# A normalisation with four times the variance and a Newton step that gives twice its result: one GpSimd scaling fewer in each of 51

## The chip, the cores and the metric

The kernel runs on one core of a Trainium2 chip. The metric is the device time in microseconds (us) of one execution; lower is better. It is one launch, all in 32-bit floats.

## The reference, cut to what matters

The input `x` has the shape 128 batches x 64 steps x 256 features. Two blocks follow each other. The first is a linear attention with a modulated output; the second a selective state-space scan (Mamba) over permuted steps. Three layer normalisations stand in them, and they are all that the change touches:

```python
def _layernorm(x, scale, bias):
    mu = jnp.mean(x, axis=-1, keepdims=True)
    var = jnp.var(x, axis=-1, keepdims=True)
    return (x - mu) * jax.lax.rsqrt(var + LN_EPS) * scale + bias      # LN_EPS = 1e-5
# block 1
xn = _layernorm(x, norm_scale, norm_bias)            # then q, k, v = xn @ W + b
...                                                  # softmaxes, k^T v, q (k^T v) -> y
h = _layernorm(y, film_norm_scale, film_norm_bias) * (1.0 + scale) + shift
x = x + silu(h) @ film_out_W + film_out_b
# block 2
h = _layernorm(x, gamma, beta) * (1.0 + scale) + shift
h = h[:, perm]
xm, z = split(h @ W_in)                              # conv over 4 steps, silu
dt = softplus(xm @ W_xp[:, :64] @ W_dt + b_dt);  Bm, Cm = xm @ W_xp[:, 64:]
hst = hst * exp(dt * A) + dt * xm * Bm;  ys = sum(hst * Cm)           # over the 64 steps, 512 x 16 states
x = x + gate * ((ys + xm * D_param) * silu(z) @ W_out)[:, inv_perm]
```

## The kernel before, in words

The 128 batches are worked in 16 groups of 8 (512 rows, four tiles of 128 rows). For a group, `prepare` (line 831) does everything up to the inputs of the scan, `scan` (line 1094) does one half of the group's state-space scan, and `finish` (line 1179) the output of that half. The first group is prepared in two parts of two tiles each (`first0`, `first2`), so there are 17 calls of `prepare`, and each calls `normalise` (line 757) three times: for `xn` from the input (line 855), for `yn` from the attention's result (line 984) and for `x1` from the first block's output (line 997). That is 51 normalisations, 45 on four tiles and 6 on two.

A normalisation has four stages. VectorE takes `bn_stats` of each tile into `st`: for the even and the odd features apart it gives a mean (`m0`, `m1`) and a sum of squares about it (`s0`, `s1`). GpSimd works on small tiles of 128 partitions x 4 (or x 2): `dm` is the difference of the two means, squared and scaled by a quarter; `ve` is the sum of squares over 256 plus epsilon; their sum is the variance. ScalarE takes the logarithm of `ve` and the exponential of minus half of it, which gives a first `r0` near the reciprocal root. GpSimd then makes one Newton step, `rt = r0 * (1.5 - 0.5 * r0 * r0 * ve)`, and the shift `mu = -mean * rt`. Last, ScalarE applies `rt` and `mu` to each tile in the four `Identity` activations.

The heavy work of a group lies elsewhere, and all engines share it. For each half of a group and each of four blocks of channels, TensorE makes the scan's input `hb` from `uT` and `diag`, ScalarE makes the decays (`decay`, eight exponentials for each buffer), VectorE runs the scan (1024 elements a partition), GpSimd or VectorE multiplies by `ct`, GpSimd adds one half of the states to the other, and TensorE folds the result into `yacc`. GpSimd also makes `diag` (line 1106) from `bT`, which ScalarE copies at line 1055 at the end of a chain of projections (`xp`, `zp`, `pd`, `bp`) of the next group.

The order of the work is written out by hand. Nothing is issued as the functions run; a planner (`Plan`, line 407 on) records every operation as a node. `order` (line 431) gives each node a due time, the later of its entry in the table `ORDER` (one list for each function, one entry for each node in the order of recording, plus 100000 for each group) and the due times of the nodes it needs:

```python
at[n] = max([ORDER[name][i] + PERIOD * g] + [at[m] for m in n.needs])
```

Nodes are then issued in the order of their due times, a little later where a buffer is missing. Each engine's queue runs strictly in that order. So the prepare of group g+1 is interleaved with the scan of group g, and the normalisations `yn` and `x1` of one group and `xn` of the next come within some 25 us of each other. Every operation passes through one line of the planner's `emit` (line 485), so the profile names nearly everything L485; the tiles' names tell the operations apart. Tables of ScalarE's functions are loaded at line 481.

Of the kernel before, what the change touches and what calls it, by code (L numbers as in the profile page):

```python
# [12 lines left out]
ALU = mybir.AluOpType  # L13
# [4 lines left out]
B, T, D, E = 128, 64, 256, 512  # L18
# [21 lines left out]
EPS = 1e-5  # L40
# [25 lines left out]
        -999921, -996486, -990765, -972941, -999936, -1000000, -999905, -999936, -999936,  # L66
        -990323, -998987, -999758, -1000000, -987539, -988111, -966277, -971501, -986083,
        -957916, -994987, -986377, -974444, -950200, -952896, -986046, -972526, -957682,
        -979289, -987850, -970490, -949297, -916289, -985408, -963837, -941730, -952038,
        -930967, -907453, -907447, -928120, -884449, -861711, -935360, -959099, -906197,  # L70
        -884745, -926919, -902673, -909643, -906909, -906200, -908429, -898155, -903063,
        -813008, -868162, -912159, -899153, -999936, -997120, -990221, -999936, -1000000,
        -999792, -826771, -682771, -989347, -990592, -990016, -992211, -992211, -978429,
        -982690, -440858, -484572, -442918, -404750, -431762, -406261, -406938, -370644, 453,
        -324628, -326712, -958581, -421254, -324629, -325398, -324629, -324629, -387488,
        -324629, -844574, -838288, -326191, -325953, -324629, -324456, -325371, -319531,
        -301212, -300329, -164417, -391164, -172529, -301121, -167816, -288749, -164473,
        -231435, -167985, -147673, -163941, -164313, -139790, -307173, -146289, -147223,
        -139567, -174994, -164473, -134847, -144594, -150226, -134317, -144822, -146906,
        -134316, -147826, -134386, -140173, -134315, -152590, -134805, -134707, -133013,  # L80
        -326287, -190004, -131686, -200375, -133015, -207481, -996027, -132927, -129988,
        -147732, -133273, -106986, -885223, -132530, -108249, -140659, -133037, -101338,
        -974289, -116497, -107952, -133014, -130547, -100436, -588731, -67587, -68642,
# [3 lines left out]
        -999784, -999756, -822479, -813355, -999773, -991829, -999405, -993980, -992161,  # L87
        -994087, -999400, -768764, -665327, -621700, -817491, -634769, -637890, -583888,
        -627342, -663883, -601358, -457294, -523956, -446498, -782722, -556542, -717683,
        -582039, -586409, -433401, -454285, -421287, -459329, -497809, -425655, -426154,  # L90
        -429164, -419967, -387487, -419719, -321626, -293880, -406937, -361628, -497357,
        -426940, -411887, -350269, -394780, -374539, -327849, -288748, -335565, -299633,
        -264048, -247552, -231344, -219423, -553809, -433515, -461393, -441827, -423327,
        -431823, -153333, -156188, -454096, -424751, -304161, -258938, -279273, -283415,
        -340857, -144850, -134706, -131268, -136899, -155056, -134271, -136435, -433892, -62033,
        -475762, -434892, -554380, -465884, -328157, -510237, -384539, -628574, -121233,
        -121771, -500934, -906743, -472740, -164647, -181881, -164481, -754360, -116569,
        -109561, -121834, -105660, -135210, -104940, -106021, -75578, -66547, -80773, -68153,
        -144505, -98818, -104252, -89186, -77436, -94044, -86891, -73823, -74895, -77276,
        -108505, -98473, -96861, -86338, -75448, -53191, -48981, -52833, -52458, -53800, -68746,  # L100
        -53712, -52940, -53192, -48477, -47718, -100418, -38381, -36696, -47354, -48108, -92558,
        -19487, -8631, -41476, -47273, -43456, -162871, -49575, -12810, -35339, -42049, -44442,
        -99823, -55773, -24279, -22535, -47650, -47276, -147956, -23424, -9283, -17974,
# [42 lines left out]
        -149966, -147998, -147736, -150000, -150000, -149540, -149273, -150000, -149489,  # L146
        -150000, -150000, -147255, -150000, -143483, -147722, -149580, -150000, -141887,
        -145855, -141886, -143290, -141594, -149567, -147693, -143761, -142133, -138763,
        -147418, -149815, -141646, -141865, -149377, -148702, -141774, -140597, -150000,
        -148702, -139206, -142860, -148144, -141417, -148704, -139302, -141567, -141330,  # L150
        -143545, -147601, -138501, -138860, -137760, -149965, -149390, -137567, -132849,
        -141748, -138950, -138764, -138744, -134769, -129564, -138764, -129760, -147721,
        -133650, -136715, -138641, -129765, -128205, -117699, -119220, -122722, -123478,
        -111005, -111004, -119884, -111271, -119852, -116230, -113143, -111005, -111114,
        -111004, -112111, -111005, -148865, -143220, -111005, -111005, -122959, -122926,
        -122986, -100655, -100656, -103176, -104256, -115077, -102238, -115728, -100658, -97964,
        -99626, -97970, -104665, -125773, -96887, -96913, -98002, -101766, -105253, -97787,
        -97126, -97126, -97126, -97126, -98335, -98054, -140963, -150000, -96888, -97126,
        -100461, -96556, -96888, -94054, -94132, -94053, -94133, -85309, -88765, -85234, -95423,
        -76351, -77623, -68358, -77139, -68709, -73881, -69122, -66121, -75878, -88439, -77322,  # L160
        -105836, -102274, -88194, -88979, -74881, -112072, -68758, -100829, -65194, -53340,
        -68359, -52170, -68869, -53341, -67392, -52171, -67165, -43786, -67246, -35127, -116295,
        -47828, -34648, -46451, -34171, -61735, -121472, -9650, -13197, -9791, -53250, -34170,
        -104935, -145568, 491, -21442, 22014, -32279, -29845, -106976, -20621, -8465, -1812,
        -19172, -29844, -36753, -25168, -3093, 7305, 15576, 11066,
# [39 lines left out]
        -150000, -148365, -149379, -148186, -147710, -148145, -150000, -147883, -147449,  # L205
        -141333, -146678, -149293, -137329, -142658, -146045, -137210, -150000, -129185,
        -138016, -129063, -150000, -122022, -137245, -146237, -134166, -119944, -107662,
        -114443, -146460, -119822, -142594, -125518, -149605, -117748, -107503, -116280,
        -115986, -101530, -105490, -101792, -108496, -111964, -113055, -119580, -142326,
        -135091, -113196, -106219, -110898, -119052, -117009, -109071, -104082, -115434,  # L210
        -101155, -101587, -101160, -102995, -101154, -121691, -107621, -118019, -98668, -103562,
        -110841, -96160, -94342, -106883, -96129, -88496, -93851, -88453, -86210, -87882,
        -73554, -79765, -149134, -125438, -137689, -117745, -149723, -145371, -73501, -77699,
        -148135, -149745, -103126, -103183, -77189, -81922, -148511, -68983, -67148, -66564,
        -71719, -56737, -55081, -61739, -55082, -60951, -49107, -56022, -47710, -75024, -47619,
        -48170, -47523, -47522, -48365, -47884, -53314, -48195, -49047, -47523, -46123, -47711,
        -73484, -55695, -47450, -44286, -47523, -47450, -44286, -42413, -42179, -41790, -41791,
        -30440, -31655, -30010, -29626, -24609, -34436, -25715, -25899, -47788, -27114, -28689,
        -26119, -35153, -29556, -27554, -27234, -69385, -44266, -44072, -24078, -27966, -20537,
        -44394, -44754, -22794, -26297, -95547, -21060, -23242, -22793, -55083, -24610, -23243,  # L220
        -19275, -23836, -34187, -16800, -21249, -15031, -14288, -111162, -13874, -6687, -22973,
        -21580, -14543, -14287, -149968, -7150, 866, -553, -314, -14542, -14286, -150000,
        -13685, 3873, 17012, 16186, -14374, -14286, -148362, -2118, 7814, 17635, 39067,
    ],
    "scan0_last": [
# [263 lines left out]
def block_kernel(  # L489
# [33 lines left out]
    pl = Plan(tc)  # L523
# [233 lines left out]
    def normalise(dst, src):  # L757
# [7 lines left out]
        mu, ve, dm = (small(a, [P, n]) for a in ("mu", "ve", "dm"))  # L765
# [12 lines left out]
        rt = small("rt", [P, n])  # L778
# [501 lines left out]
```

## Time and profile before

| | us |
|---|---|
| device time, median of 3 runs (lowest to highest) | 1947.62 (1947.34 to 1949.36) |
| device time of the profiled execution | 1950.4 |
| its span, first to last instruction | 1948.7 |
| TensorE busy (matmuls) | 1825.3 |
| GpSimd busy | 1788.3 |
| VectorE busy | 1776.0 |
| ScalarE busy | 1698.9 |
| the 51 scalings `dm<-dm` by a quarter on GpSimd, by their durations | 8.8 + 1.2 |

PE is TensorE's matmuls, PEld its weight loads, DVE VectorE, ACT ScalarE, POOL GpSimd. In a row of the groups, `out<-in` are the tiles written and read, then their shapes and how many there are, then the busy time, the mean duration of one in ns, and the engine's idle time just ahead of them with what ended most of it. In a row of the timeline the first number is the start in us from the span's start and the second the length of the row; a row may merge several like instructions, and square brackets give the idle time ahead and who ended it. A wait row names the waiting engine and tile, the one that released it, the total in us, the number of waits and the longest. The profiled execution is the one in which all these are measured; its device time is 2.8 us above the median of the runs.

### The profile page before, as it was taken

The numbers are of one execution on the slowest core, as the hardware profiler recorded it, in microseconds if no ns is written. First come the engines' busy times: TensorE is split into PE (matmuls) and PEld (weight loads), VectorE is DVE, ScalarE is ACT, GpSimd is POOL, SyncE is SP. The second block draws the span as 40 slices with busy tenths as digits, with TensorE's granted clock in tenths as the row PEclk, the third lists the DMA queues.
The fourth block names the chain that finished last, engine by engine and source line by source line (L and its number), as shares of the span: only waits on it lengthen the run. The fifth ranks groups of instructions, "written<-read, shape, count | busy, mean of one in ns | idle before, by whom it ended". The sixth has DMA issues, their size and how long they took to land. (4 is left out here: it accounts for less than half of the span.)

```text
span 1948.7 us, 32432 instructions
## 1 busy us (share of the span) xinstructions
PE 1825.3 (94%) x11304; PEld 931.1 (48%) x11304; DVE 1776.0 (91%) x1626; ACT 1698.9 (87%) x3981; POOL 1788.3 (92%) x1519
## 2 busy tenths in 40 slices
PE   6798999999999999999999999999999999999777
PEld 5453544545455454545535454453545445454233
DVE  5589799999999999999999999999999999999796
ACT  5889799898989989899998989889898998989762
POOL 3579799999999999999999999999999999999997
PEclk9899999999999999999999999999999999999898
DMA  4211322204122221412213132220412222041220
GB/s 142 80 50 45 85 72 73 82 23 120 39 86 64 67 87 28 112 54 85 64 56 88 38 103 61 81 68 28 115 39 86 72 68 84 23 114 36 82 65 22
DMA packets 173083, 135.71 MB, mean 70 GB/s; under 512 B 30804, under 2 KB 157000, under 8 KB 172920
## 3 DMA queue, kind: packets, MB, share of 16 engines
q1 hardware_dynamic: 172920, 133.64, 23.7%
q8 instruction: 90, 1.47, 0.3%
q14 instruction: 73, 0.60, 0.1%
HBM read 98.84 MB, written 34.75 MB: 69 GB/s over the span
## 5 line engine op out<-in xcount | busy, mean ns | idle before, releaser
L485 DVE TENSOR_TENSOR_SCAN hs<-decay,hb 128x1024 f32<-128x1024 f32 x384 | 864.0, 2276 | 69.4 <-PE hb L485 21.8
L485 ACT ACTIVATE decay<-dt,nA 128x252 f32<-128x252 f32 x2048 | 859.2, 503 | 77.1 <-DMA dt<-dt_d 40.5
L485 POOL TENSOR_TENSOR hs<-hs,ct 128x1024 f32<-128x1024 f32 x384 | 900.1, 2366 | 20.6 <-DVE hs L485 16.2
L485 PE MATMUL hb<-diag,uT 64*64 64x512 f32 x4096 | 534.5, 619 | 67.9 <-DVE hs L485 63.0
L485 POOL TENSOR_TENSOR hs<-hs 128x1024 f32<-128x1024 f32 x224 | 526.6, 2364 | 13.8 <-DVE hs L485 9.9
L485 DVE TENSOR_TENSOR_SCAN hb<-decay,hb 128x1024 f32<-128x1024 f32 x128 | 291.7, 2279 | 0.0
L485 PE MATMUL yacc<-hs,fold 128*64 128x256 f32 x2304 | 283.5, 387 | 4.3 <-ACT yacc L485 2.2
L485 PEld LDWEIGHTS hb<-diag,uT 64*64 64x64 f32 x4096 | 122.1, 133 | 294.7 <-DVE hs L485 125.6
L485 PEld LDWEIGHTS yacc<-hs,fold 128*64 128x64 f32 x2304 | 163.3, 137 | 123.3 <-issue 49.7
L481 ACT ACT_TABLE_LOAD x160 | 205.3, 1283 | 3.5 <-PEq L1268 0.8
L485 DVE TENSOR_TENSOR hs<-hb,ct 128x1024 f32<-128x1024 f32 x128 | 156.3, 1221 | 5.1
L485 DVE SCALAR_TENSOR_TENSOR xz<-xp,vec,xz 128x504 f32<-128x504 f32 (+5 forms) x204 | 140.8, 701 | 12.1 <-ACT xz L485 7.5
L485 POOL TENSOR_TENSOR diag<-fold,bT 128x1024 f32<-128x1024 f32 x64 | 122.1, 1909 | 10.3 <-ACT bT L485 10.3
L485 PE MATMUL zp<-h,win 128*128 128x512 f32 (+1 forms) x272 | 123.4, 580 | 1.6 <-DVE xz L485 0.6
L485 PE MATMUL xp<-h,win 128*128 128x512 f32 (+1 forms) x272 | 118.3, 578 | 2.1 <-DVE xz L485 1.1
L485 PE MATMUL yop<-wout,xz 128*128 128x256 f32 x512 | 117.6, 383 | 0.0
L485 PEld LDWEIGHTS yop<-wout,xz 128*128 128x128 f32 x512 | 94.7, 190 | 25.1 <-ACT decay L485 10.6
L485 POOL TENSOR_TENSOR w<-dt,xz 128x512 f32<-128x512 f32 (+1 forms) x68 | 81.7, 1212 | 12.9 <-ACT dt L485 12.4
L485 ACT ACTIVATE yacc<-xz,vec 128x256 f32<-128x256 f32 x128 | 60.1, 470 | 32.7 <-PE yacc L485 32.7
L485 PEld LDWEIGHTS xp<-h,win 128*128 128x128 f32 x272 | 50.7, 192 | 68.8 <-issue 50.7
L485 PEld LDWEIGHTS zp<-h,win 128*128 128x128 f32 x272 | 48.6, 189 | 62.4 <-issue 43.5
L485 ACT ACTIVATE hT<-htp,mods 128x64 f32<-128x64 f32 x256 | 77.9, 441 | 0.2
(138 smaller groups left out, 2358.8 us busy)
## 6 DMA issues: line engine op xcount, KB each, us to landing
ct<-c_d SPq DMA_DIRECT2D x128, 256.0 KB
dt<-dt_d SPq DMA_DIRECT2D x256, 128.0 KB
dt_d<-dt SPq DMA_DIRECT2D x60, 256.0 KB
ga<-gate_d SPq DMA_DIRECT2D x64, 128.0 KB
xr<-x_d SPq DMA_DIRECT2D x32, 256.0 KB
out<-xr SPq DMA_DIRECT2D x32, 256.0 KB
xt<-in_x SPq DMA_DIRECT2D x15, 512.0 KB
x_d<-xt SPq DMA_DIRECT2D x15, 512.0 KB
```

The source lines that it names most:

```text
L481: engine.preload_act_table_set(loaded)
L485: getattr(engine, method)(*real, **kreal)
```

## The change

The quarter ahead of the sum goes: `ve` becomes four times the variance (and four times epsilon), so `dm` squared is added as it is. ScalarE's `r0` is then half the reciprocal root, and the Newton step with the constants -1 and 3 in place of -0.5 and 1.5 gives twice its usual result, which is the reciprocal root itself. One instruction of GpSimd is left out in each normalisation; two others get other constants.

```diff
         pl.gpsimd.tensor_tensor(dm, m0, m1, op=ALU.subtract)
         pl.gpsimd.tensor_tensor(ve, s0, s1, op=ALU.add)
         pl.gpsimd.tensor_tensor(dm, dm, dm, op=ALU.mult)
-        pl.gpsimd.tensor_scalar(ve, ve, 1.0 / D, EPS, op0=ALU.mult, op1=ALU.add)
-        pl.gpsimd.tensor_scalar(dm, dm, 0.25, 0.0, op0=ALU.mult, op1=ALU.add)
+        pl.gpsimd.tensor_scalar(ve, ve, 4.0 / D, 4.0 * EPS, op0=ALU.mult, op1=ALU.add)
         pl.gpsimd.tensor_tensor(ve, ve, dm, op=ALU.add)
         r0 = small("r0", [P, n])
         pl.scalar.activation(r0, ve, AF.Ln)
...
         pl.gpsimd.tensor_tensor(rt, r0, r0, op=ALU.mult)
         pl.gpsimd.tensor_tensor(rt, rt, ve, op=ALU.mult)
-        pl.gpsimd.tensor_scalar(rt, rt, -0.5, 1.5, op0=ALU.mult, op1=ALU.add)
+        pl.gpsimd.tensor_scalar(rt, rt, -1.0, 3.0, op0=ALU.mult, op1=ALU.add)
         pl.gpsimd.tensor_tensor(rt, rt, r0, op=ALU.mult)
```

The table `ORDER` loses the entries of the nodes that are gone, three in each of the lists `first0`, `first2`, `second` and `prepare` (so 172 entries become 169, and 202 become 199); every other entry keeps its value. The start of `prepare`:

```diff
     "prepare": [
         -150000, -150000, -143902, -149054, -149244, -148364, -149973, -150000, -148365,
-        -150000, -148365, -149379, -148186, -147710, -148145, -150000, -147883, -147449,
+        -150000, -148365, -148186, -147710, -148145, -150000, -147883, -147449, -141333,
```

## The prediction, made before the changed kernel was run

> **What bounds the kernel now.** I read the page first: busy shares, the 40 slices, the groups. They show no single bound.
>
> ```profile
> PE   6798999999999999999999999999999999999777
> DVE  5589799999999999999999999999999999999796
> ACT  5889799898989989899998989889898998989762
> POOL 3579799999999999999999999999999999999997
> ```
>
> From the seventh slice (290 us) to the 37th, TensorE, VectorE and GpSimd all stand at nine tenths; ScalarE is just under. So a busy share names no bound; the order of the hand-overs must. In the page's chain that ended last there is nothing before 1803 us, so I followed the hand-overs by hand through the timeline of one group, 1128 to 1243 us. GpSimd's `diag` that waits for `bT` marks the same place in every group: it starts at 1127.95 and 1243.14, 115.19 us apart. The list of waits comes next.
>
> ```profile
> ACT r L485 <- POOL ve L485: 58.4, 36, 6.8
> POOL diag L485 <- ACT bT L485: 10.3, 13, 0.8
> ```
>
> ScalarE waits for the normalisations' `ve` 36 times, 58.4 us in all, and GpSimd waits for ScalarE's `bT` once a group. So GpSimd hands to ScalarE, and ScalarE back to GpSimd. What lies between is shown by the timeline of the group.
>
> ```profile
> 1164.59 0.20 POOL L485 TENSOR_TENSOR dm<-st 128x4 f32<-128x4 f32 x1 [0.20 <-DVE st L485]
> 1164.74 0.21 POOL L485 TENSOR_TENSOR ve<-st 128x4 f32<-128x4 f32 x1
> 1164.89 0.20 POOL L485 TENSOR_TENSOR dm<-dm 128x4 f32<-128x4 f32 x1
> 1165.19 0.20 POOL L485 TENSOR_SCALAR ve<-ve 128x4 f32<-128x4 f32 x1
> 1165.47 0.20 POOL L485 TENSOR_SCALAR dm<-dm 128x4 f32<-128x4 f32 x1
> 1165.75 0.20 POOL L485 TENSOR_TENSOR ve<-ve,dm 128x4 f32<-128x4 f32 x1
> 1165.90 0.20 POOL L485 TENSOR_TENSOR mu<-st 128x4 f32<-128x4 f32 x1
> ...
> 1189.43 0.20 ACT L485 ACTIVATE r<-ve 128x4 f32<-128x4 f32 x1 [0.95 <-POOL ve L485]
> ...
> 1191.31 2.07 ACT L485 ACTIVATE x<-xt,mu,rt 128x256 f32<-128x256 f32 x4 [0.25 <-POOL mu L485]
> ...
> 1193.43 1.60 PE L485 MATMUL gtp<-gsel,x 128*128 128x128 f32 x12 [0.17 <-ACT x L485]
> ...
> 1196.63 2.29 DVE L485 TENSOR_TENSOR_SCAN hs<-decay,hb 128x1024 f32<-128x1024 f32 x1 [0.88 <-ACT decay L485]
> ...
> 1243.14 1.90 POOL L485 TENSOR_TENSOR diag<-fold,bT 128x1024 f32<-128x1024 f32 x1 [0.78 <-ACT bT L485]
> ```
>
> The reader is to see a ring. From 1164.59 (`dm` of `yn`) to 1192 GpSimd is never released by another engine: it works through `yn` (1164.59 to 1167.8), large multiplications, and `x1` with `xn` interleaved (1186.57 to 1192.3). ScalarE waits 0.95 us for the last `ve` and 0.25 us for `mu`. From there ScalarE stands in unbroken work until `bT` at 1242.84, save for a wait of 0.17 us later. TensorE (0.17), VectorE (0.88) and finally GpSimd (0.78) wait for it. The other side closes it: TensorE waits 0.43 us for ScalarE's `xz` at 1222.02 and then runs without a stop to the `hb` for which VectorE waits 0.30 us at 1248.76; in the group before, the same VectorE stretch (from 1133.57, with one wait of 0.32 us for TensorE's `ap`) ends in the `st` for which GpSimd waits 0.20 us at 1164.59. All three normalisations of a group lie on this ring.
>
> **The change part by part.** *The instruction that goes* is the row `dm<-dm` at 1165.47. Its duration is 0.20 us (the two groups of them: 45 of 196 ns and 6 of 196 ns, with 3.6 and 0.4 us idle ahead of them). But its place in the queue is longer: 1165.19, 1165.47, 1165.75 are starts 0.28 us apart, while a following independent instruction starts 0.15 us on (1165.75, 1165.90). After the change `ve<-ve,dm` follows `ve<-ve`, on which it depends as it depends on the squared `dm`, so one step of 0.28 us goes, not 0.15: that is my value, since before and after the next neighbour is a dependent one. In the interleaved pair, `x1` at 1187.16, 1187.43 and `xn` at 1188.65, 1188.92, the step is 0.27. The Trainium skill's page "Perfetto Trace Analysis", section "GPSIMD Engine Instruction", says that the span reported for a GpSimd instruction can't be relied on and that starts of consecutive instructions should be used. The rows bear that out: neighbours' spans overlap (1165.75 + 0.20 is past 1165.90) where they are independent, and have gaps where they aren't. By the reported spans the 51 instructions would come to 10.0 us, by the spacing to 14.3 us.
>
> *The two other constants* are operands of instructions that stay; 0 us. *The order*: the lists lose just the entry of the node that goes, and a due time is the later of the entry and the needs. The entry decides for its successor in one list alone, `second`, -147736 against -147998 for `ve`, a shift of 0.26 us of plan time in one group, and no other node of GpSimd or ScalarE lies between. So every queue keeps its order, no DMA and no wait is moved, and nothing is added.
>
> *What lies on the path.* Thirteen times (yn at 243, 358, 473 ... 1627 us, each with `x1` and `xn` some 22 us later) three scalings lie on the ring: 3 x 0.277 = 0.83 us a time. Whether all of it comes through hangs on what is late next, which for the case of 1189 us can be read:
> - VectorE's own way to 1196.63 has a slack of 0.88 us, just above 0.83.
> - TensorE's `hb` at 1190.67 follows VectorE (1.71 us of waiting, which GpSimd does not touch); then `rp` and `gtp`. `gtp` starts at 1192.66, and its end gains at most some 0.43 us: the `hb` after it starts at 1194.97, where 1192.66 and the 1.88 us of an unhindered `gtp` (1769.54 to 1771.42, where it waits for nothing) give 1194.54. But the second `xtp`, 1198.94, waits again for ScalarE's `h`: `yacc` ahead of it takes 2.32 us in place of 1.88 to 1.95, so TensorE catches up the missing 0.4 us there.
> So I take the whole 0.83 us in the ten groups like this one. In three (610 to 620, 1071 to 1081, 1303 to 1313 us) the granted clock is 0.83 in a window of 10 us just here, where the other ten show 1.00. The `gtp` then takes 2.91 to 3.14 us and TensorE, not ScalarE, sets the second `xtp`. Groups between two `diag` marks last 114.83 us at the least; the two that hold a single such window, 115.59 and 115.35 (one without it, 782 to 898 us, lasts 115.62, so the clock isn't the only cause). So 0.5 to 0.76 us of another delay lies beside the ring there, and of 0.83 us I count 0.25.
>
> The sum, against the profiled execution of 1950.4 us: ten groups x 0.83 = 8.3; three x 0.25 = 0.8; the last group's `yn` and `x1` (1742, 1764 us) 2 x 0.28 = 0.55; the first half's `xn`, `yn`, `x1` (6, 29, 49 us), where ScalarE waits 6.8, 2.8 and 1.4 us for `ve`, all on the serial start, 3 x 0.28 = 0.85; the seven others between 26 and 200 us, where GpSimd also waits up to 5.9 us for VectorE, at half, 1.0. Together **11.5 us**: 1938.9 in that execution, which is 2.8 above the median of 1947.62, so **1936.1** as a median. Floor and ceiling of what is not known: none of it comes through (0), or all 51 steps do (14.3 us) and the three slow-clock windows go away as well (3 x 0.6 = 1.8): 1931.5.
>
> **The rivals.**
> 1. *TensorE's way through `gtp` is late next.* If the catch-up at `xtp` doesn't happen, a group gains the 0.43 us that TensorE can gain there. For it: `gtp`'s wait is only 0.17 us in the row shown, and TensorE is busy without a pause afterwards. Against: the stretched `yacc`. 10 x 0.43, nothing in the three slow-clock groups, and 1.6 of start and end: 5.9 us, 1941.7.
> 2. *The wait only changes hands.* If the ring is closed by VectorE or TensorE work that I haven't seen as such, ScalarE's waits for `ve` (0.95 and 2.3 us a group) and GpSimd's for `st` and `bT` grow by what is saved, and the gain stays at the start, 1 to 2 us: 1946. For it: TensorE, VectorE and GpSimd are each idle only some 4 to 5 us a group. That the change moves an instruction's work to its neighbour and so saves only the 0 to 0.15 us of dispatch would look much the same.
> 3. *Slower: the clock.* A window at the lower clock falls on the same pause of TensorE in 3 of 13 groups; it is seen as 0.66 over 1075 to 1080 us, which is 1.7 us of TensorE's work. If a tighter ScalarE chain moved the pause so that it is caught in all 13, and TensorE became the bound with the full 1.7 us on the path, the ten new ones cost 17 us against 11.5 gained: 1953. It decides from nine new windows on ((11.5 + 3.9) / 1.7). Against it: the pause itself, 1.71 us before the `hb` at 1190.67, comes from VectorE and keeps its length, and `gtp`'s wait gets shorter. The skill's page "TensorE: Matmul & The Clock Gate", section "What's actually happening", says that the clock is lowered after an idle window of about 3.4 us that runs free of the kernel; no idle time of TensorE that long stands in these rows, so by the page the pause would cost nothing, and where the windows fall would be chance.
>
> **How the numbers follow.** The forecast has 62%, rival 1 20%, rival 2 14%, rival 3 4%. The predicted time is the forecast's, 1936.1. The range takes in the forecast with the bound of 1931.5 and rival 1 (1941.7) with some 2 us for its own spread: 1931.5 to 1944, which leaves out rivals 2 and 3, 18%. About 0.2%, 3.9 us, is what a measurement of this kernel can tell from no change. Faster by more: forecast and rival 1, 82%; within: rival 2, 14%; slower by more: 4%.
>
> **What would show it.** GpSimd has 51 instructions fewer (1468) and 10 us less busy time. `ve<-ve,dm` starts 0.28 us after `ve<-ve`. The marks of `diag` lie some 114.0 us apart in an undisturbed group, against 114.83. GpSimd's waits for `bT` (0.79) and `st` (0.2) stay as they are; VectorE's 0.88 shrinks to near 0.05. If the step is mis-sized, the waits of ScalarE for `ve` keep their length and the marks move by less; under rival 1 TensorE's wait at `gtp` is gone and no stretched `yacc` is left; under rival 2 the waits grow by 0.8 us a group. I am wrong most easily in the slack: 0.88 against 0.83 us is a hair, read in one group.

## The result, and the profile after

The changed kernel takes 1939.48 us (median of five, 1936.99 to 1942.74) against 1947.62 us (five, 1945.41 to 1951.31) of the kernel before on the same chip: a ratio of 0.9959, with a 95% interval from 0.9944 to 0.9974. That is 8.1 us less, where 11.5 were forecast. Beside two more sets of runs of the kernel before, the changed kernel gave 0.9950 [0.9933, 0.9968] and 0.9937 [0.9923, 0.9951], by the medians 9.7 and 12.6 us less. Its profiled execution took 1942.74 us, its span 1941.0: 7.7 us less than the profiled one of before.

The page of the changed kernel, in 40 slices, shows the same picture as before, since no busy share tells of a ring:

```profile
PE   7799999999999999999999999999999999999777
...
DVE  4589799999999999999999999899999999999796
ACT  4889799898989989899898989889898998989762
POOL 3589799999999999999999999999999999999997
```

Its list of waits (engine and tile that waits, who released it, total in us, how often, the longest):

```profile
ACT r L485 <- POOL ve L485: 44.4, 32, 6.2
...
POOL dm L485 <- DVE st L485: 34.5, 19, 5.9
...
POOL diag L485 <- ACT bT L485: 10.2, 13, 0.8
```

ScalarE's wait for the normalisations' `ve` fell from 58.4 to 44.4 us; GpSimd's wait for `bT` stayed at 13 times 0.79.

The timeline of the changed kernel, at the places that were shown of before (start, length, engine, tiles, and in brackets the idle time ahead with who ended it):

```profile
1161.10 0.20 POOL L485 TENSOR_TENSOR dm<-st 128x4 f32<-128x4 f32 x1 [0.20 <-DVE st L485]
...
1161.70 0.20 POOL L485 TENSOR_SCALAR ve<-ve 128x4 f32<-128x4 f32 x1
1161.98 0.20 POOL L485 TENSOR_TENSOR ve<-ve,dm 128x4 f32<-128x4 f32 x1
1162.13 0.20 POOL L485 TENSOR_TENSOR mu<-st 128x4 f32<-128x4 f32 x1
...
1183.49 0.19 POOL L485 TENSOR_SCALAR ve<-ve 128x4 f32<-128x4 f32 x1
1183.77 0.21 POOL L485 TENSOR_TENSOR mu<-st 128x4 f32<-128x4 f32 x1
1183.92 0.20 POOL L485 TENSOR_TENSOR ve<-ve,dm 128x4 f32<-128x4 f32 x1
...
1184.82 0.19 POOL L485 TENSOR_SCALAR ve<-ve 128x4 f32<-128x4 f32 x1
1185.10 0.20 POOL L485 TENSOR_TENSOR ve<-ve,dm 128x4 f32<-128x4 f32 x1
...
1185.33 0.21 ACT L485 ACTIVATE r<-ve 128x4 f32<-128x4 f32 x1 [0.37 <-POOL ve L485]
...
1187.20 2.08 ACT L485 ACTIVATE x<-xt,mu,rt 128x256 f32<-128x256 f32 x4 [0.24 <-POOL mu L485]
...
1189.17 1.95 PE L485 MATMUL gtp<-gsel,x 128*128 128x128 f32 x16
...
1192.52 2.29 DVE L485 TENSOR_TENSOR_SCAN hs<-decay,hb 128x1024 f32<-128x1024 f32 x1 [0.26 <-ACT decay L485]
...
1192.65 2.13 PE L485 MATMUL yacc<-hs,fold 128*64 128x256 f32 x16
...
1238.99 1.90 POOL L485 TENSOR_TENSOR diag<-fold,bT 128x1024 f32<-128x1024 f32 x1 [0.79 <-ACT bT L485]
```

Of the kernel before, the first normalisation of the pair, and TensorE's `yacc`:

```profile
1187.16 0.19 POOL L485 TENSOR_SCALAR ve<-ve 128x4 f32<-128x4 f32 x1
...
1187.43 0.19 POOL L485 TENSOR_SCALAR dm<-dm 128x4 f32<-128x4 f32 x1
1187.58 0.21 POOL L485 TENSOR_TENSOR mu<-st 128x4 f32<-128x4 f32 x1
...
1187.74 0.20 POOL L485 TENSOR_TENSOR ve<-ve,dm 128x4 f32<-128x4 f32 x1
...
1196.57 2.32 PE L485 MATMUL yacc<-hs,fold 128*64 128x256 f32 x16
```

Here is where the time went. The yn at 1161 us has its sum 0.28 us after `ve<-ve`, where it was 0.56 (1165.19 to 1165.75). In the pair, the first normalisation is xn (of the next group) and the second is x1; the prediction named the two the other way round. x1's sum (1185.10) also comes 0.28 after `ve<-ve`. In xn, however, `mu<-st` has moved into the free place, so the sum comes 0.43 after `ve<-ve` (before, 1187.16 to 1187.74, it was 0.58): 0.15 saved, not 0.28. Together 0.28 (yn) + 0.27 (x1, where it was 0.55) + 0.15 (xn) = 0.70 us a group. ScalarE's wait for the last `ve` is 0.58 us shorter, TensorE no longer waits in `gtp`, and VectorE's wait for `decay` shrank from 0.88 to 0.26.

The `diag` marks give it for the whole execution:

| distances of the 13 marks, us | shortest | all twelve together | first mark | from the last mark to the end |
|---|---|---|---|---|
| before | 114.83 | 1383.86 | 321.67 | 243.2 |
| changed | 114.13 | 1377.89 | 321.98 | 241.1 |
| changed, second profile (a later run) | 114.16 | 1377.24 | 319.99 | 242.1 |
| changed, third profile (a later run) | 114.15 | 1376.18 | 321.53 | 239.9 |

The shortest distance fell by 0.67 to 0.70 us. The twelve together lost 6.0 to 7.7 us; twelve times 0.70 would be 8.4. Two distances of the first profile grew: the sixth (115.47, before 114.83) and the ninth (117.99, before 116.65). In each lies a spell at half the clock (at 958 and at 1255 us) that the kernel before doesn't have there. The timeline of TensorE in the sixth:

```profile
956.53 1.09 PE L485 MATMUL hb<-diag,uT 64*64 64x512 f32 x8 [1.71 <-DVE hs L485]
957.55 1.68 PE L485 MATMUL rp<-yo,gsel 128*128 128x256 f32 x4
959.02 3.09 PE L485 MATMUL gtp<-gsel,x 128*128 128x128 f32 x16
```

Against 1.13 and 1.95 us for the same `rp` and `gtp` at 1188 to 1191 us, the spell costs TensorE 1.7 us; the group's mark comes some 1.3 us later than in an undisturbed group (114.13).

One more wait tells how long a group is. Some 9 us behind its mark, ScalarE's `decay` waits for `dt`, which has gone out to memory and comes back by DMA. In the changed kernel's fourth and fifth group (114.14 and 114.99 us):

```profile
673.62 2.88 ACT L485 ACTIVATE decay<-dt,nA 128x252 f32<-128x252 f32 x7 [1.17 <-DMA dt<-dt_d]
...
788.61 2.88 ACT L485 ACTIVATE decay<-dt,nA 128x252 f32<-128x252 f32 x7 [2.03 <-DMA dt<-dt_d]
```

In groups at the shortest distance this wait is 0.9 to 1.2 us. Where it is longer, and no spell at half the clock lies in the group, the distance is the shortest one plus what the wait has above 1.17 us: here 114.13 + 0.86 = 114.99, and in the kernel before 114.83 + 0.78 = 115.61, measured 115.62 (782 to 898 us). Over the twelve profiles this holds within 0.04 us in 110 of 112 such groups (the first of each profile is left out; it is 0.1 to 0.5 us longer than that); in 101 of them the profile puts the wait down to this DMA, in the others to VectorE's `qm` or `qt`. In the sixth group a wait of 1.41 us takes 0.24 of the 1.34 us and leaves 1.1 for the spell. So a group lasts as long as the ring, plus a late `dt`, plus a spell. The change shortened the first by 0.67 to 0.70; the other two differ from profile to profile, and the sum over the twelve distances with them. No run altered the trip of `dt`, so its part is read from the rows and not tested.

### The profile page after: what moved, and what is told of

The parts are those of the page before. It is cut to its first block, busy times and chain, and to the rows that moved or that the text cites. A ratio compares the mean times of both kernels' runs of the same rounds, so it can differ in the third digit from the quotient of the medians.

```text
span 1941.0 us, 32381 instructions
## 1 busy us (share of the span) xinstructions
PE 1819.4 (94%) x11304; PEld 931.0 (48%) x11304; DVE 1775.8 (91%) x1626; ACT 1696.5 (87%) x3981; POOL 1778.1 (92%) x1468
## 5 line engine op out<-in xcount | busy, mean ns | idle before, releaser
L485 POOL TENSOR_TENSOR hs<-hs,ct 128x1024 f32<-128x1024 f32 x384 | 899.5, 2363 | 19.9 <-DVE hs L485 14.8
L485 POOL TENSOR_TENSOR diag<-fold,bT 128x1024 f32<-128x1024 f32 x64 | 122.0, 1907 | 10.2 <-ACT bT L485 10.2
```

The costliest lines, as they stand in the source:

```text
L485: getattr(engine, method)(*real, **kreal)
```

## The experiments

The theory, **A**: what counts is GpSimd time ahead of the sums that release ScalarE, since ScalarE's chain sets the pace of a group. A rival, **B**: GpSimd is full, and its time counts wherever it lies. Another, **C**: something else is late next, so only a part comes through. All marks below are the shortest distance between two `diag`; in the two kernels that were profiled more than once it differs by 0.03 to 0.04 us.

**The changed kernel again.** No edit.

> The changed kernel as it is, timed again. Both theories: 5 to 11 us under the kernel before. What it tells apart is the spread: if the start of the trace and the groups with a lower granted clock differ from execution to execution, the shortest distance of two diag marks is again 114.13 us (0.02 either way) while the first diag mark and the longer distances move by up to 2 us. If instead the change itself moved the start by 1 us (the dm at 243.07 us before stood at 244.17 after), the first marks come at the same place as in the first profile.

Measured: 1940.68 us (1934.54 to 1948.66, seven runs), ratio 0.9950; marks 114.16. The gain is there again, with marks 0.03 us from the first; the first mark moved by 2.0 us, and single executions scatter by several us.

**The quarter left out in one normalisation only** (one execution each). The edit, for one of the three sites:

```diff
+        f = 4.0 if site == here else 1.0
-        pl.gpsimd.tensor_scalar(ve, ve, 4.0 / D, 4.0 * EPS, op0=ALU.mult, op1=ALU.add)
+        pl.gpsimd.tensor_scalar(ve, ve, f / D, f * EPS, op0=ALU.mult, op1=ALU.add)
+        if site != here:
+            pl.gpsimd.tensor_scalar(dm, dm, 0.25, 0.0, op0=ALU.mult, op1=ALU.add)
...
+        a, b = (-1.0, 3.0) if site == here else (-0.5, 1.5)
-        pl.gpsimd.tensor_scalar(rt, rt, -1.0, 3.0, op0=ALU.mult, op1=ALU.add)
+        pl.gpsimd.tensor_scalar(rt, rt, a, b, op0=ALU.mult, op1=ALU.add)
```

> The quarter left out in yn alone. Theory A (the normalisations lie one behind the other on the ring and each gives what its own place in GpSimd's queue gives: 0.28 in yn, 0.15 in x1, where an independent mu stands behind it, 0.27 in xn): the shortest distance of two diag marks is 114.83 - 0.28 = 114.55 us. Theory B (all three steps are alike and a slack of 0.70 us caps their sum): also 114.55. Theory C (GpSimd's time as such counts, 0.155 us a place): 114.68.

> The quarter left out in x1 alone. Theory A: 114.83 - 0.15 = 114.68 us between two diag marks at the least. Theory B (each step is worth 0.27 to 0.28 alone, and only the sum of three is capped): 114.56. Theory C: 114.68.

> The quarter left out in xn alone. Theory A: 114.83 - 0.27 = 114.56 us. Theory B: 114.56. Theory C: 114.68. With the other two, A wants the three gains to add up to 0.70, B to 0.83, C to 0.45.

| quarter left out in | time, us | marks | less than before's 114.83 |
|---|---|---|---|
| yn | 1949.08 | 114.60 | 0.23 |
| x1 | 1948.42 | 114.45 | 0.38 |
| xn | 1948.54 | 114.58 | 0.25 |
| all three (the changed kernel, in the same comparison; before 1950.41) | 1940.68 | 114.16 | 0.67 |

The expectations for x1 and xn carry the swapped names: the one with the 0.15 us step is xn. The stretch on GpSimd itself, from the pair's first `dm` to x1's `mu`, got 0.30 us shorter by x1's quarter and 0.18 by xn's (4.52 us before, 4.22, 4.34), which bears out a small step in xn. The marks say that each of the three shortens the ring. But with the names put right they lie 0.05 (yn), 0.11 (x1) and 0.10 us (xn) from what A wanted, more than they vary from profile to profile, and their sum (0.86) is above the 0.67 to 0.70 that the three bring together. The runs don't explain this. The cap on the sum that B supposed is not the answer: the last two kernels below go beyond 0.70. The times, of single executions, tell nothing here.

**The same GpSimd work in two places.** Three scalings by 1.0 more in each xn, once ahead of the sum, once behind the pair's last instruction; the order of every queue is that of the changed kernel.

```diff
+            for _ in range(3):                     # ahead
+                pl.gpsimd.tensor_scalar(dm, dm, 1.0, 0.0, op0=ALU.mult, op1=ALU.add)
             pl.gpsimd.tensor_tensor(ve, ve, dm, op=ALU.add)
...
             pl.gpsimd.tensor_tensor(mu, mu, rt, op=ALU.mult)
+            for _ in range(3):                     # or behind
+                pl.gpsimd.tensor_scalar(dm, dm, 1.0, 0.0, op0=ALU.mult, op1=ALU.add)
```

> The changed kernel with three more scalings of dm by 1.0 on GpSimd in xn alone, one behind the other, ahead of the sum ve<-ve,dm. GpSimd gets 3 x 0.28 = 0.83 us more work in each group, and the second sum of the pair (x1's) comes that much later. Theory A (the place counts: GpSimd's sums release ScalarE, and ScalarE's bT releases GpSimd's diag): all of it is on the ring, the diag marks lie 114.13 + 0.83 = 114.96 us apart in the shortest group, ScalarE's wait for the last ve of the pair grows from 0.37 to 1.2 us, VectorE's wait for decay from 0.26 to some 1.0; time 13 x 0.83 + 1 to 2 at the start = 11 to 13 us above the changed kernel, 1951 to 1953. Theory B (GpSimd is full and its time as such counts, wherever it lies): the same 11 to 13 us here, and the same again in the kernel that has the three scalings behind mu. Theory C (it is late-next limited already, TensorE or VectorE set the group): 0.26 us of the 0.83 is swallowed, 114.7, time 1947 to 1949.

> The changed kernel with the same three scalings in xn alone, but behind mu<-mu,rt, the last instruction of the pair, so that ScalarE has all it waits for before they run. Theory A (the place counts): the large products behind them start 0.83 us later, which GpSimd's waits for DVE hs (about 0.5 us) and for bT (0.79 us) take in; bT's wait shrinks to near nothing, the marks stay within 0.2 us of 114.13, time 0 to 3 us above the changed kernel, 1940 to 1943. Theory B (GpSimd's time as such counts): as with the scalings ahead of the sum, marks 114.96, 1951 to 1953.

| | time, us | ratio to before | marks | POOL instructions |
|---|---|---|---|---|
| ahead of the sum | 1950.37 (10 runs) | 0.9999 [0.9987, 1.0011] | 114.95 | 1519 |
| behind | 1944.03 (9 runs) | 0.9966 [0.9954, 0.9978] | 114.38 | 1519 |

Both have as many GpSimd instructions as the kernel before, and GpSimd is as busy in both (1787.7 and 1787.1 us). Ahead of the sum, the whole 0.82 us arrives in the marks and the gain is gone; behind, 0.25 us arrives (a little more than the 0.2 that A allowed, and 1944.03 is 1 us above its range). B, which wanted the same in both, is out, and so is C, which wanted 114.7 ahead of the sum. In the timeline of the kernel with the scalings ahead, the waits for GpSimd's sum and behind it have grown (from 0.37, 0 and 0.26; A had put the first at 1.2):

```profile
1191.04 0.20 ACT L485 ACTIVATE r<-ve 128x4 f32<-128x4 f32 x1 [0.74 <-POOL ve L485]
...
1195.04 1.60 PE L485 MATMUL gtp<-gsel,x 128*128 128x128 f32 x12 [0.36 <-ACT x L485]
...
1198.23 2.29 DVE L485 TENSOR_TENSOR_SCAN hs<-decay,hb 128x1024 f32<-128x1024 f32 x1 [1.07 <-ACT decay L485]
```

In that of the kernel with the scalings behind, ScalarE's waits are those of the changed kernel, and the delay takes a second way:

```profile
1186.23 0.21 ACT L485 ACTIVATE r<-ve 128x4 f32<-128x4 f32 x1 [0.38 <-POOL ve L485]
...
1189.02 0.74 POOL L485 TENSOR_SCALAR dm<-dm 128x4 f32<-128x4 f32 x3
...
1189.72 4.68 POOL L485 TENSOR_TENSOR hs<-hs 128x1024 f32<-128x1024 f32 x2
...
1194.45 1.94 PE L485 MATMUL yacc<-hs,fold 128*64 128x256 f32 x14 [0.26 <-POOL hs L485]
1196.07 1.22 DVE L485 TENSOR_TENSOR hs<-hb,ct 128x1024 f32<-128x1024 f32 x1 [0.36 <-PE yacc L485]
```

The reader is to see that GpSimd's `hs` starts 0.70 us later behind the scalings (1189.02 to 1189.72), that TensorE's `yacc` now waits for it, and VectorE for `yacc`: a quarter of a microsecond of it reaches the ring. Most of the rest is taken in where GpSimd waits for VectorE: those waits total 24.1 us in the changed kernel and 17.6 here.

```profile
POOL hs L485 <- DVE hs L485: 17.6, 29, 3.0
...
POOL diag L485 <- ACT bT L485: 10.2, 13, 0.8
```

The second line is a miss of the expectation: the wait for `bT` was to shrink and did not. Some 5.5 us ahead of `diag`, VectorE releases GpSimd's `hs` (after a wait of 0.54 us in the changed kernel, at 1233.52), and from there to `diag` it is 5.47 us in both kernels (1233.52 to 1238.99, 1234.68 to 1240.15). So what GpSimd loses or gains before that release doesn't reach `bT`'s wait, and its 0.79 us is no measure of slack.

**Three more instructions left out.** The kernel leaves out the difference of the two means, so its variance lacks that part.

```diff
-        pl.gpsimd.tensor_tensor(dm, m0, m1, op=ALU.subtract)
         pl.gpsimd.tensor_tensor(ve, s0, s1, op=ALU.add)
-        pl.gpsimd.tensor_tensor(dm, dm, dm, op=ALU.mult)
         pl.gpsimd.tensor_scalar(ve, ve, 4.0 / D, 4.0 * EPS, op0=ALU.mult, op1=ALU.add)
-        pl.gpsimd.tensor_tensor(ve, ve, dm, op=ALU.add)
```

> The changed kernel without the difference of the two means: dm, its square and the sum are left out in all 51 normalisations, so the variance lacks the part that comes from the difference of the means of even and odd features. GpSimd has 153 instructions fewer, some 0.7 us in each normalisation, 2.0 us in a group, nearly three times what the change saved. Theory A (the ring has a slack that is now nearly used up): VectorE's wait for decay, 0.26 us in the changed kernel, goes to nothing and no more comes through; marks not under 113.85 us, time 13 x 0.26 + 2 at the start = some 5 us below the changed kernel, 1934 to 1937; GpSimd's waits for st and bT grow by 1.7 us a group, ScalarE's wait for the last ve goes. Theory B (GpSimd's time counts): 13 x 2.0 + 3 = 29 us less, marks 112.1, time near 1911. Between the two: TensorE or VectorE follow partly, since their own waits in other places shrink too; marks near 113.3, time near 1928.

Measured: 1935.17 us (four runs), ratio 0.9915 [0.9895, 0.9936]; marks 113.68. By the starts, 1.3 us of GpSimd's work goes from a group (0.59 in yn, 0.75 in the pair; by busy time 21.9 us in all), not the 2.0 of the expectation. Of it 0.45 comes through (A expected 0.26 at most, B all). In its timeline GpSimd has met the next limit, VectorE's `st` for x1, and VectorE's `hs` has no wait for `decay` left:

```profile
1186.06 2.29 DVE L483 TENSOR_TENSOR_SCAN hs<-decay,hb 128x1024 f32<-128x1024 f32 x1
...
1294.22 1.07 DVE L483 BATCH_NORM_STATS2 st<-xt 128x6 f32<-128x256 f32 x3
...
1295.37 0.20 POOL L483 TENSOR_TENSOR ve<-st 128x4 f32<-128x4 f32 x1 [0.29 <-DVE st L483]
```

What GpSimd saves turns into waiting for VectorE: for `hs` 37.3 us in place of 24.1, for `st` 36.8 in place of 34.5. The expectation had put it at `st` and `bT`; `bT` again stayed (10.3).

**The same work in another order.** xn's two `mu` instructions come behind x1's Newton step, by two entries in `ORDER`.

```diff
     "prepare": [
...
-        (entries 14 and 15)  -150000, -147883,
+        (entries 14 and 15)  -144270, -144270,
```

> The changed kernel with only two entries of the due times altered: xn's mu<-st and mu<-mu come behind x1's Newton step, in place of between xn's instructions; the work is the same. In the changed kernel the two take 0.31 us between ve* of xn and the first instruction of x1. Theory A: x1's first instruction then meets its st, which VectorE ends 0.2 us before that instruction starts now, so it gets a wait for st and the pair's last sum comes only 0.1 to 0.2 us earlier; marks 113.95 to 114.05, time 1 to 3 us below the changed kernel, 1937 to 1939. Theory B (each step ahead of the sum comes through in full): marks 113.82, 4 us below, 1936. Theory C (nothing more to be had on this path, or the mu are late for xn's own activations): no difference or up to 2 us more.

Measured: 1939.14 us (five runs), ratio 0.9935 [0.9922, 0.9947]; marks 113.99, 0.14 less than the changed kernel, as A had it, and the time at the edge of its range. In its timeline x1's `dm` starts 0.07 us after the end of the last `bn_stats` (1178.15 + 1.08), as in the kernel above (1295.29 to 1295.37), and 0.32 us after the sum ahead of it, where an independent instruction follows a sum after 0.15. So VectorE's `st` seems to hold it here too, though by too little to be listed as a wait:

```profile
1178.15 1.08 DVE L487 BATCH_NORM_STATS2 st<-xt 128x6 f32<-128x256 f32 x3
...
1179.30 0.20 POOL L487 TENSOR_TENSOR dm<-st 128x4 f32<-128x4 f32 x1
...
1180.41 0.21 ACT L487 ACTIVATE r<-ve 128x4 f32<-128x4 f32 x1 [0.24 <-POOL ve L487]
```

This is the one version of the same computation that may be better than the changed kernel, so it was run once more beside it, on one chip:

> The changed kernel once more, beside the one with xn's mu behind x1's Newton step, on one chip: 1938 to 1941. Theory A (the diag marks tell the time: each 0.1 us a group is 1.3 us): it stands 1 to 3 us above the other one. Theory B (the two entries of the due times bring nothing): within 1 us of it.

> The kernel with xn's mu<-st and mu<-mu behind x1's Newton step once more. Theory A: shortest distance of the marks again 0.14 us under the changed kernel's (113.99 against 114.13), time 1937 to 1939, 1 to 3 us under it. Theory B: within 1 us of it, and the lower time of the first run came from its chip and where the windows of the lower clock fell.

Measured: the changed kernel 1941.47 us (six runs, 1939.36 to 1943.71), 0.9937 [0.9923, 0.9951]; with the `mu` late 1936.65 (five runs, 1934.85 to 1941.48; a sixth took 3404.76 us, which nothing here explains, and is left out), 0.9915 [0.9899, 0.9931]; marks 114.15 and 114.03. Its two medians (1939.14, 1936.65) stand 0.3 to 4.8 us below the changed kernel's three (1939.48 to 1941.47), and its marks are 0.10 to 0.17 us shorter, which over 13 groups is 1.3 to 2.2 us. But the intervals of the pair overlap, so it is likely better than the changed kernel and not shown to be; against the kernel before, both its intervals lie clear of 1.

## Why the prediction was right, and where not

*The ring: right.* Instructions ahead of the sum move the marks in full (0.82 of 0.83 us), the same ones behind it by 0.25. Of its closing link, the wait for `bT`, the runs show less than was said: it keeps its 0.79 us in every kernel, whatever GpSimd gains or loses before VectorE's release. And the prediction left out `dt`'s way through memory, which lengthens every group in which it comes back late; the group that it read, 1128 to 1243 us, is one of these (a wait of 1.57 us, 115.19). Without what its wait had above 1.17, that group went from 114.79 to 114.13 us (115.09 and 2.13 after), so the step came off there as well.

*The step of 0.28 us: the term that was mis-sized.* It holds in yn and x1 (0.28, 0.27) and not in xn (0.15), where `mu<-st` takes the free place and then itself starts 0.28 us after its predecessor. So three steps are worth 0.70 us, not 0.83, and ten groups 7.0, not 8.3; with the other terms left as they were the sum is 10.2. The prediction had looked at which instruction the next one depends on, but for xn not at which instruction the queue puts next. The Trainium skill's page "Perfetto Trace Analysis", section "GPSIMD Engine Instruction", has GpSimd's instructions timed by the spacing of their starts, not by their spans. Here three spans of 0.20 would make 0.60, the three old spacings 0.83, and measured are 0.70: neither gives the number, only the spacing of the new neighbours does.

*No queue changes its order: right.* In the profiles every engine has the same instructions in the same order but for the 51; GpSimd has 1468 instructions and 1778.1 us, 10.2 less.

*The slack on VectorE: right in place, not used up.* 0.88 became 0.26, not 0.05, as the chain moved by 0.62 there. Nothing else was late first. The kernel without `dm` shows how near the end is: 1.3 us a group less on GpSimd brings 0.45, as VectorE's `st` is late next.

*TensorE's catch-up (rival 1): rightly turned down.* `gtp`'s wait is gone (the row has all 16 in one), the `yacc` behind it is still stretched (2.13, before 2.32), and the marks moved by 0.70, not 0.43.

*The wait changes hands (rival 2): no*, but for a part: over the whole execution ScalarE's wait for `ve` fell by 14.0 to 14.8 us in the three profiles, while its wait for VectorE's `hs` ahead of `decay` grew by 3.7 to 4.9 us (from 22.1) and GpSimd's for `st` by 1.2 to 2.8 (from 31.7).

*The clock (rival 3): no, but the three groups were not to be fixed either.* Between the first mark and the last, before had three spells at half the clock, all behind the 1.71 us pause; the changed kernel has one there (the sixth group, in all three of its profiles) and once another behind `qtp`. So the pause wasn't caught oftener. Of the three groups for which the prediction allowed 0.25 us in place of the full step, two have no spell in any of the three profiles, the third (the ninth) has one in the first profile alone, behind `qtp`, and the sixth is disturbed instead.

The Trainium skill's page "TensorE: Matmul & The Clock Gate", section "What's actually happening", has the clock lowered after an idle window of about 3.4 us, and these windows run free of the kernel. The profiles' records of the granted clock bear out the windows: within each of the twelve profiles all spells begin whole multiples of 3.41 us apart. They don't bear out that a window has to be idle throughout. The pause of 1.71 us stands 144 times between the marks of these profiles. The 13 that were caught are just those that began 0.18 to 0.60 us behind the edge of a window, as counted from the spells of the same profile; of the other 131 none began there. A group of 114.13 us is 33.4 windows, so the pause drifts through the window from group to group and is caught now and then; all 13 at once, as the rival has it, would need groups of a whole number of windows.

*Start and end: not told apart.* 1.85 us were forecast for the start, and first marks at 319.99 to 321.98 against 321.67 show -0.3 to 1.7. The first and the third profile have a spell at a lower clock at 25 to 30 us (0.66 over these 5 us); the second, whose mark comes first, has none, and before has none either. The pair without a spell gives 1.7 us, near the term, but it is one pair, and the spell makes as much difference as the term itself.

So the mechanism was right and the forecast 3.4 us too large by the first comparison, of which 1.3 us is xn's step. The three comparisons gave 8.1, 9.7 and 12.6 us less; their mean, 10.2, is what the sum gives with xn's step put right. That it comes out so close is in part luck, as the comparisons differ among themselves by 1.6 to 4.5 us; `dt`, the spells and the start are what the profiles show to differ between executions of one kernel.

## What to carry to other kernels

Where every engine is nine tenths busy, as here, an instruction's price is its place: ask which hand-over it stands ahead of, and test it with the same work put once ahead of that hand-over and once behind. Work out the price of a removed small instruction from the starts of those that will be neighbours afterwards, not from those that it had. A delay on the ring passed in full here (0.82 of 0.83 us), a gain only until the next engine was late: after this change, 1.3 us a group of further GpSimd work left out brought 0.45. And before a difference between groups or runs is put down to a change, look for a wait that tells it: here one wait for memory gave the length of a group to 0.04 us.

## What the runs showed that was not expected

- A GpSimd instruction on 128 x 4 elements starts 0.15 or 0.27 to 0.30 us after the one before it, and dependence on that one isn't the whole rule: `mu<-st`, which waits for nothing new, starts 0.28 us after `ve<-ve` (1183.49, 1183.77) and 0.15 after the sum in yn (1161.98, 1162.13). The runs don't show why.
- The kernel before had medians of 1947.62, 1950.41, 1951.10 and 1954.06 us in four comparisons, the changed one 1939.48, 1940.68 and 1941.47. The ratio of one comparison moves by 0.002, a third to half of the gain.
- TensorE's clock falls to 0.50 for 3.41 us, beginning 1.1 to 1.5 us after the end of a pause of only 1.71 us (in the rows above the pause ends at 956.53, the half clock lasts from 958.0 to 961.4; in the kernel before from 615.5 to 618.9, behind a pause ending at 614.21), and behind some pauses at `qtp` (one of 2.37 us that ends at 1253.40, half clock from 1255.0). The same pause is in every group, but only none to three groups of a profile have a spell. What tells them from the others without exception is where the pause begins in the 3.41 us window. In the three profiles of the changed kernel it was caught in the same group, having begun 0.21 to 0.31 us behind an edge; why three executions stand alike to the windows stays open.
- The ninth distance of the marks is the longest in every kernel (116.1 to 118.4 us), with and without a spell at the lower clock in it. It is the group in which ScalarE's `decay` waits longest for `dt`: 2.6 to 3.9 us in the twelve profiles, eleven times put down to that DMA (3.35 in the changed kernel's second, where 114.16 + 2.18 gives the measured 116.34). Why the wait is longest in that group stays open.
